# Layer 0's context attention and its FFN in one phase of a two-layer decoder kernel

## The chip, the cores and the metric

The kernel runs on one core of a Trainium2 chip. The metric is the device time of one execution in microseconds (us). The engines are named as the profile names them: PE (TensorE matmul), PEld (TensorE weight load), DVE (VectorE), ACT (ScalarE), POOL (GpSimd), SP (SyncE, which here only issues DMAs; its queue is SPq).

## The reference, cut to what matters

A decoder of two layers over 8 batches of 512 tokens of width 256, all float32. Each sublayer is followed by a residual add and a layer norm. The change touches two sublayers of layer 0: attention over a context of 64 keys per batch, and an FFN whose two butterfly transforms the kernel folds into its two weight matrices beforehand.

```python
# x: (8, 512, 256)   ctx: (8, 64, 256)
x = layernorm(x + L0_attn(x))                      # self attention, 16 heads of 16

def L0_xattn(q, k, v, mask):                       # q = x, k = v = ctx, 16 heads of 16
    sim = einsum('bhqd,bhkd->bhqk', q, k) / sqrt(16)
    sim = sim + (-1e9) * (1 - mask)
    out = einsum('bhqk,bhkd->bhqd', softmax(sim), v)
    return out                                     # heads side by side, no projection
x = layernorm(x + L0_xattn(x, ctx, ctx, mask))

def L0_ffn(x):
    h = x @ W_exp + b_exp                          # 256 -> 1024
    h = gelu(butterfly(h, up_weights) + up_bias)
    h = butterfly(h, down_weights)
    return h @ W_con + b_con + down_bias           # 1024 -> 256
x = layernorm(x + L0_ffn(x))
# layer 1: causal self attention (16 heads of 64), attention over tokens and context,
# and a mixture of 8 experts (2 per token) that scatters tokens into rows by expert
```

## The kernel before

The kernel is one program traced in Python. Instructions of one engine run in their order in that engine's queue. That order is set when the program is built: a planner walks the traced instructions, those traced earlier having priority, and gives an engine the next one that its own estimate of times calls ready, so an instruction can stand ahead of work that was traced before it. At run time nothing is reordered, and an engine whose next instruction isn't ready waits.

Activations stay in SBUF as `xs[b]`, one tile of 128 x (4 x 256) per batch, and each sublayer overwrites it. Tiles come from pools. A *phase* is a pool that is opened for one stage; where its tiles lie over tiles of an earlier phase, each waits for the tiles that it lies over (`reuse_waits="tile"`). The pool `routing` (variable `keep`) is an ordinary one and is opened after layer 0's FFN; it holds the small tables of the expert routing and the zero tile from which the expert rows in DRAM (`rows_in`, 64 DMAs from SP, line 781) are cleared. PSUM, from this point on, is split into three kinds of tiles with two buffers each: `s` (two banks; scores, hidden units, Q/K), `t` (one bank; transposes) and `o` (one bank; products).

`_pipeline(units, stages, later)` runs a list of units through stages, one step apart: in step n stage k works on unit n - k. After the stages of each step it runs one piece of the list `later`.

**Context attention** (phase `l0_context`, lines 637 to 724). A unit is a block of 128 queries of a batch, so there are 32 units, and four stages:

- `l0x_pre`, once per batch: x transposed to `xT` (8 transposes on PE, copied out by DVE and ACT); `bd`, the keys spread block-diagonally so that 8 heads are one matmul (2 POOL multiplies, line 643); the mask by DMA (`mi`, line 650) turned into a bias; `v2`, the values of head pairs with zeros between them (a POOL memset, line 654, and two DMAs, line 656). `bd` uses the tag `att` of the pool `work`, which the self attention ahead of it and other stages use too.
- `l0x_scores`: two matmuls of 512 columns (line 666, each recorded as two) into an `s` tile; then on DVE scale and bias (675), row maxima (683), subtraction (684); Exp on ACT (685); sums on DVE (686).
- `l0x_transposes`: 8 transposes of the probabilities (696), copied out half by DVE (94) and half by ACT (96).
- `l0x_values`: 8 narrow matmuls with `v2` (705, 16 records); reciprocal, scaling (711) on DVE, residual on POOL (717); after a batch's last unit the norm (199 to 209), which writes `xs[b]`.

**FFN** (phase `l0_ffn`, lines 727 to 763). First the down weights are transposed (`wdn`, line 761). Then a pipeline over the 8 batches with two stages. `ffn_up` transposes `xs[b]`, makes 8 blocks of 128 hidden units in four `s` tiles (line 738, 32 records per batch), and applies Gelu on ACT (747) into `g`, a tile of 16 KB per partition with two buffers. `ffn_down` multiplies by `wdn` (`project_and_norm`, line 225, 64 records per batch) into `o` tiles, adds x plus the bias row (232), and norms.

Layer 1's self attention (`l1_self`, lines 783 to 912) follows. It is a pipeline over 256 units (batch, head pair, query block) in which Q, K and V of the next head pair are made while the present one is worked on. The rotary turn of Q and K ends with four accumulating DMAs from POOL per head pair (`qk<-turned`, line 810), for which that pair's first scores (855) wait.

The DMAs of layer 1's attention weights (lines 625 to 634) are traced just before the context attention.

Of the kernel before, what the change touches and what calls it, by code (L numbers as in the profile page):

```python
# [11 lines left out]
F32 = mybir.dt.float32  # L12
I32 = mybir.dt.int32
AF = mybir.ActivationFunctionType
ALU = mybir.AluOpType
# [3 lines left out]
P = 128  # L19
S = 512  # L20
D = 256
S2 = 64
NT = S // P
KC = D // P
# [3 lines left out]
BLK = 256  # L28


def _pipeline(units, stages, later=None):


    units = list(units)
    for step in range(len(units) + len(stages) - 1):
        for k, stage in enumerate(stages):
            if 0 <= step - k < len(units):
                stage(*units[step - k])
        if later:
            later.pop(0)()  # L40
    while later:
        later.pop(0)()

# [2 lines left out]
def decoder_kernel(ctx: ExitStack, tc: tile.TileContext, a: dict, out: bass.AP):  # L46
    nc = tc.nc
    NB = a["x"].shape[0]
# [23 lines left out]
    def phase(name):  # L72

        return tc.tile_pool(name=name, bufs=2, side="right", reuse_waits="tile")
# [10 lines left out]
    def o_tile(name):  # L85
        return pp["o"].tile([P, 512], F32, tag="o", name=name)
# [35 lines left out]
    def rows(w):  # L122

        return w.rearrange("(c p) n -> p c n", p=P)
# [62 lines left out]
    def x_transposed(b):  # L187
        xT = work.tile([P, KC, S], F32, tag="xT", name="xT")
        transposed(xT, xs[b])
        return xT  # L190

    def normed(dst, r, on_act=False):

        st = work.tile([P, NT, 6], F32, tag="st", name="st")
        mv = work.tile([P, NT, 2], F32, tag="mv", name="mv")
        ve = work.tile([P, NT], F32, tag="ve", name="ve")
        rs = work.tile([P, NT], F32, tag="rs", name="rs")
        for i in range(NT):
            dve.bn_stats(st[:, i, :], r[:, i, :])  # L199
            dve.bn_aggr(mv[:, i, :], st[:, i, :])  # L200
        dve.tensor_scalar(ve, mv[:, :, 1], LN_EPS, None, ALU.add)
        pool.tensor_tensor(rs, ve, mhalf, ALU.pow)
        if on_act:
            dve.scalar_tensor_tensor(ve, mv[:, :, 0], -1.0, rs, ALU.mult, ALU.mult)
        for i in range(NT):
            if on_act:
                act.activation(dst[:, i, :], r[:, i, :], AF.Identity, bias=ve[:, i : i + 1], scale=rs[:, i : i + 1])
                continue
            dve.tensor_scalar(
                dst[:, i, :], r[:, i, :], mv[:, i, 0:1], rs[:, i : i + 1], ALU.subtract, ALU.mult  # L210
            )

    def r_tile():
        return work.tile([P, NT, D], F32, tag="r", name="r", bufs=1)

    def project_and_norm(b, lhs, w, n, plus, later=None):

        r = r_tile()

        def piece(i2):  # L220
            o = o_tile("o_out").rearrange("p (i n) -> p i n", i=2)
            for j in range(2):
                i = 2 * i2 + j
                for c in range(n):
                    pe.matmul(  # L225
                        o[:, j, :],
                        lhsT=lhs[:, c, i * P : (i + 1) * P],
                        rhs=w[:, c, :],
                        start=(c == 0),
                        stop=(c == n - 1),  # L230
                    )
            dve.tensor_tensor(r[:, 2 * i2 : 2 * i2 + 2, :], o, plus[:, 2 * i2 : 2 * i2 + 2, :], ALU.add)
            if i2 == NT // 2 - 1:
                normed(xs[b], r)

        for i2 in range(NT // 2):
            if later is None:
                piece(i2)
            else:
                later.append(partial(piece, i2))  # L240
# [101 lines left out]
    live = {}  # L342
# [191 lines left out]
    with tc.tile_pool(name="bfly", bufs=1, side="right") as bfly, phase("l0_self") as ph, psum("a", 3, 1, 1):  # L534
# [25 lines left out]
        later = []  # L560
# [60 lines left out]
    cs = tabs[:, 0:1024].rearrange("p (t n) -> p t n", t=2)  # L621
    causal = tabs[:, 1024:1536]


    sp.dma_start(out=wqT, in_=rows(a["at_wqT"]))
    sp.dma_start(out=wkdT, in_=rows(a["at_wkdT"]))
    sp.dma_start(out=wkuT, in_=a["at_wkuT"])
    sp.dma_start(out=wvuT, in_=a["at_wvuT"])

    sp.dma_start(out=cs[:, 0, :], in_=a["rope"][0])  # L630
    for h in range(0, P, 32):
        sp.dma_start(out=cs[h : h + 32, 1, :], in_=a["rope"][1][h ^ 32 : (h ^ 32) + 32, :])
    sp.dma_start(out=causal, in_=a["causal"])
    sp.dma_start(out=woT1, in_=rows(a["at_woT"]))

    def l0x_pre(b, i):
        if i:
            return
        xT = x_transposed(b)

        bd = work.tile([P, KC, 8, S2], F32, tag="att", name="bd")
        for c in range(KC):
            pool.tensor_tensor(
                bd[:, c],
                ctxT[:, c, b * S2 : (b + 1) * S2].unsqueeze(1).to_broadcast([P, 8, S2]),
                hmask.unsqueeze(2).to_broadcast([P, 8, S2]),
                ALU.mult,
            )
        mi = ph.tile([P, NT, S2], I32, tag="mi", name="mi")
        sp.dma_start(out=mi, in_=a["mask"][b].rearrange("(i p) k -> p i k", p=P))  # L650
        bias = ph.tile([P, NT, S2], F32, tag="bias", name="bias")
        dve.tensor_scalar(bias, mi, 1.0, 1.0e9, ALU.subtract, ALU.mult)
        v2 = ph.tile([P, 8, 32], F32, tag="v2", name="v2")
        pool.memset(v2, 0.0)
        for j in range(2):
            sp.dma_start(
                out=v2[64 * j : 64 * (j + 1), :, 16 * j : 16 * (j + 1)],
                in_=a["ctx"][b * S2 : (b + 1) * S2, :].rearrange("k (h two n) -> k h two n", two=2, n=16)[:, :, j, :],
            )
        live["xT", b], live["bd", b], live["bias", b], live["v2", b] = xT, bd, bias, v2  # L660

    def l0x_scores(b, i):
        xT, bd, bias = live["xT", b], live["bd", b], live["bias", b]
# [35 lines left out]

    def l0x_values(b, i):  # L700
        pt, sums = live.pop(("pt", b, i))
        v2 = live["v2", b]
        o = o_tile("o_xpv")
        for h in range(8):
            pe.matmul(o[:, h * 32 : (h + 1) * 32], lhsT=pt[:, h, :], rhs=v2[:, h, :], start=True, stop=True)
        rsum = col("rsum16", 16)
        dve.reciprocal(rsum, sums)
        if i == 0:
            live["r", b] = r_tile()
        r = live["r", b]  # L710
        dve.tensor_tensor(
            r[:, i, :].rearrange("p (h n) -> p h n", h=16),
            o[:, 0:D].rearrange("p (h n) -> p h n", h=16),
            rsum.unsqueeze(2).to_broadcast([P, 16, 16]),
            ALU.mult,
        )
        pool.tensor_tensor(r[:, i, :], r[:, i, :], xs[b][:, i, :], ALU.add)
        if i == NT - 1:
            normed(xs[b], r)

    with phase("l0_context") as ph:
        _pipeline(
            [(b, i) for b in range(NB) for i in range(NT)], [l0x_pre, l0x_scores, l0x_transposes, l0x_values]
        )


    def big_tile(name, bufs=1):
        return ph.tile([P, 8, S], F32, tag="big", name=name, bufs=bufs)

    def ffn_up(b):  # L730
        xT = x_transposed(b)
        g = big_tile("g", 2)
        for f2 in range(4):
            s = s_tile("s_h")
            for j in range(2):
                f = 2 * f2 + j
                for c in range(KC):
                    pe.matmul(
                        s[:, j, :],
                        lhsT=wup[:, c, f * P : (f + 1) * P],  # L740
                        rhs=xT[:, c, :],
                        start=(c == 0),
                        stop=(c == KC - 1),
                    )
            for j in range(2):
                f = 2 * f2 + j
                act.activation(g[:, f, :], s[:, j, :], AF.Gelu, bias=upb[:, f : f + 1])
        xb = work.tile([P, NT, D], F32, tag="att", name="xb")
        pool.tensor_tensor(xb, xs[b], dnb.unsqueeze(1).to_broadcast([P, NT, D]), ALU.add)
        live["g", b] = g, xb  # L750

    def ffn_down(b):
        g, xb = live.pop(("g", b))
        project_and_norm(b, g, wdn, 8, xb)

    with phase("l0_ffn") as ph:
        wdn = ph.tile([P, 8, D], F32, tag="wdn", name="wdn", bufs=1)
        for f in range(0, 8, 2):
            t = t_tile("tW")
            for j in range(4):  # L760
                pe.transpose(t[:, j, :], wdnT[:, j % 2, (f + j // 2) * P : (f + j // 2 + 1) * P], ident)
            evac(wdn[:, f : f + 2, :].rearrange("p f n -> p (f n)"), t.rearrange("p j n -> p (j n)"))
        _pipeline([(b,) for b in range(NB)], [ffn_up, ffn_down])

# [75 lines left out]
            dve.tensor_scalar(p[:, j, 0:n], p[:, j, 0:n], rsum[:, j : j + 1], None, ALU.mult)  # L842

    put_off = []

    def nothing(*_):
        pass

    def l1_scores(b, c, i):
        q, k, _ = live["qkv", b, c]  # L850
# [545 lines left out]
```

## Time and profile before

| what | value |
|---|---|
| time, median of 3 runs | 4053.77 us (4045.73 to 4060.90) |
| profiled execution | 4058.26 us, its span 4056.5 us |
| PE busy over the span | 3799.6 us (94%) |
| DVE / ACT / POOL busy | 2195.0 / 1418.2 / 1098.8 us |
| mean granted TensorE clock | 0.947 |
| context attention, 912 to 1146 us of the span | PE busy 203.54, DVE busy 217.56 of 234 us, clock 0.75 |
| FFN, 1158 to 1384 us | PE busy 225.96, DVE busy 44.44 of 226 us, clock 1.00 |
| loads of an activation table on ACT | 4 in the whole span, 1283 ns each |

A busy PE is not PE at full speed: the table gives the clock that was granted beside it. The profile names a group by source line, engine, operation and tiles; a line can be that of a helper (184 transposes, 94 and 96 copies out of PSUM, 199 to 209 the norm). [...]

### The profile page before, as it was taken

The numbers are of one execution on the slowest core, as the hardware profiler recorded it, in microseconds if no ns is written. First come the engines' busy times: TensorE is split into PE (matmuls) and PEld (weight loads), VectorE is DVE, ScalarE is ACT, GpSimd is POOL, SyncE is SP. The second block draws the span as 40 slices with busy tenths as digits, with TensorE's granted clock in tenths as the row PEclk, the third lists the DMA queues.
The fourth block names the chain that finished last, engine by engine and source line by source line (L and its number), as shares of the span: only waits on it lengthen the run. The fifth ranks groups of instructions, "written<-read, shape, count | busy, mean of one in ns | idle before, by whom it ended". The sixth has DMA issues, their size and how long they took to land. (4 is left out here: it accounts for less than half of the span.)

```text
span 4056.5 us, 58011 instructions
## 1 busy us (share of the span) xinstructions
PE 3799.6 (94%) x22164; PEld 2393.7 (59%) x22164; DVE 2195.0 (54%) x6177; ACT 1418.2 (35%) x2980; POOL 1098.8 (27%) x974
## 2 busy tenths in 40 slices
PE   8999999998999999999999999999999995999995
PEld 3333333346656655666566665666666664888884
DVE  5666656558942377777777765555555553000002
ACT  2443343442221254444544433333333331222222
POOL 4767566652211122211211110110101101122222
PEclk8999899997789999999999999999999997999997
DMA  3000011119500122222322220000000001766664
GB/s 120 25 22 22 22 32 32 32 52 236 124 6 1 32 37 32 32 32 32 40 35 32 32 32 1 17 13 10 12 17 17 17 11 40 243 183 182 182 183 107
DMA packets 173432, 236.12 MB, mean 58 GB/s; under 512 B 26554, under 2 KB 138618, under 8 KB 173155
## 3 DMA queue, kind: packets, MB, share of 16 engines
q1 hardware_dynamic: 146562, 179.93, 14.6%
q0 software_dynamic: 26592, 52.49, 9.0%
q8 instruction: 175, 2.87, 0.3%
q14 instruction: 103, 0.84, 0.1%
HBM read 136.78 MB, written 62.03 MB: 49 GB/s over the span
## 5 line engine op out<-in xcount | busy, mean ns | idle before, releaser
L417 DVE CUSTOM_DVE_ANT_0 scored<-s_sc,decay 128x512 f32<-128x512 f32 x512 | 323.4, 687 | 293.4 <-PE s_sc L412 291.9
L470 ACT ACTIVATE pt<-s_st 128x1024 f32<-128x1024 f32 x256 | 261.4, 1024 | 373.0 <-PE o_pv L481 224.9
L810 POOL DMA_DIRECT2D qk<-turned x256 | 202.6, 1207 | 627.0 <-issue 273.0
L96 ACT COPY pt<-tP 128x128 f32<-128x128 f32 (+2 forms) x480 | 224.3, 467 | 384.2 <-PE tP L279 299.2
L279 PE MATMUL tP<-ident,p 128*128 128x128 f32 x2304 | 355.5, 287 | 2.3 <-DVE pt L94 0.8
L279 PEld LDWEIGHTS tP<-ident,p 128*128 128x128 f32 x2304 | 250.6, 143 | 145.8 <-issue 74.0
L269 ACT ACTIVATE p<-p,nm 128x128 f32<-128x128 f32 (+3 forms) x512 | 283.0, 555 | 145.4 <-DVE nm L267 145.4
L983 ACT ACTIVATE p<-s_sc,nm 128x576 f32<-128x576 f32 x256 | 189.6, 743 | 348.9 <-DVE nm L982 348.9
L1287 DVE TENSOR_SCALAR y<-o_y,share 128x256 f32<-128x256 f32 x78 | 34.2, 479 | 491.8 <-PE o_y L1265 491.8
L842 DVE TENSOR_SCALAR p<-p,rsum 128x576 f32<-128x576 f32 (+4 forms) x768 | 295.4, 428 | 6.1
L1249 PE MATMUL s_h<-xnT,we 128*128 128x256 f32 x1248 | 284.7, 381 | 2.8 <-DMA we<-in_mo_w 2.8
L412 PE MATMUL s_sc<-k,q 32*128 32x512 f32 x1024 | 267.5, 703 | 16.4 <-ACT k L398 14.0
L94 DVE COPY pt<-tP 128x128 f32<-128x128 f32 (+2 forms) x480 | 259.1, 540 | 42.5 <-PE tP L279 28.6
L257 DVE CUSTOM_DVE_ANT_0 p<-s_sc,tabs 128x128 f32<-128x128 f32 (+3 forms) x512 | 234.9, 484 | 84.9 <-PE s_sc L855 84.9
L855 PE MATMUL s_sc<-qk 64*128 64x128 f32 (+3 forms) x1024 | 265.8, 486 | 12.3 <-DVE turned L807 8.2
L1265 PE MATMUL o_y<-we,h 128*128 128x256 f32 x1248 | 275.6, 379 | 0.0
L1265 PEld LDWEIGHTS o_y<-we,h 128*128 128x128 f32 x1248 | 237.1, 190 | 32.2
L1249 PEld LDWEIGHTS s_h<-xnT,we 128*128 128x128 f32 x1248 | 232.6, 191 | 32.2 <-DMA we<-in_mo_w 3.2
L982 DVE TENSOR_REDUCE nm<-s_sc 128x1 f32<-128x576 f32 x256 | 183.6, 749 | 119.1 <-PE s_sc L981 119.1
L1288 POOL DMA_INDIRECT total<-y,to x78 | 121.2, 1554 | 458.5 <-DVE y L1287 295.1
L891 PE MATMUL o_pv<-pt,vc 128*64 128x128 f32 x2560 | 221.8, 284 | 0.0
L1007 PE MATMUL o_pv<-pt,vc 128*64 128x128 f32 x2048 | 197.7, 287 | 0.0
(248 smaller groups left out, 6476.1 us busy)
## 6 DMA issues: line engine op xcount, KB each, us to landing
we<-in_mo_w SPq DMA_DIRECT2D x78, 1024.0 KB, 5.7
rows_in<-zero SPq DMA_DIRECT2D x64, 530.0 KB, 11.2
qk<-turned POOLq DMA_DIRECT2D x256, 128.0 KB, 4.4
xr<-rows_in SPq DMA_DIRECT2D x39, 265.0 KB, 6.2
coef<-in_ff_upw SPq DMA_DIRECT2D x40, 256.0 KB, 3.2
coef<-in_ff_dnw SPq DMA_DIRECT2D x40, 256.0 KB, 3.1
x<-in_x SPq DMA_DIRECT2D x8, 512.0 KB, 9.4
total<-x SPq DMA_DIRECT2D x8, 512.0 KB, 2.9
```

What stands on the lines that cost most here:

```text
L94: dve.tensor_copy(dst, src)
L96: act.copy(dst, src)
L257: dve.tensor_tensor_reduce(out=p[:, j, 0:n], in0=s[:, j, 0:n], in1=m, scale=1.0, scalar=-3.0e38, op0=op, op1=reduced, accum_out=mx[:, j : ...
L269: act.activation(p[:, j, 0:n], p[:, j, 0:n], AF.Exp, bias=nm[:, j : j + 1], scale=scale, accum_out=sums[:, at + j : at + j + 1],)
L279: pe.transpose(t[:, k, :], p[:, j, k * P : (k + 1) * P], ident)
L412: pe.matmul(s[:, j, :], lhsT=q[h : h + 32, i * P : (i + 1) * P], rhs=k[h : h + 32, :], start=True, stop=True)
L417: dve.tensor_tensor_reduce(out=scored[:, h, :], in0=s[:, j, :], in1=decay[:, i, :], scale=1.0, scalar=-3.0e38, op0=ALU.mult, op1=ALU.max, ...
L470: act.activation(pt, s, AF.Exp, scale=1.0 / 16.0)
L842: dve.tensor_scalar(p[:, j, 0:n], p[:, j, 0:n], rsum[:, j : j + 1], None, ALU.mult)
L855: pe.matmul(s[:, j, 0:n], lhsT=q[h : h + 64, i * P : (i + 1) * P], rhs=k[h : h + 64, 0:n], start=True, stop=True)
L1249: pe.matmul(s[:, j, :], lhsT=w1[:, c, f * P : (f + 1) * P], rhs=xnT[:, c, :], start=(c == 0), stop=(c == KC - 1),)
L1265: pe.matmul(o[:, i, :], lhsT=h[:, f, i * P : (i + 1) * P], rhs=w2[:, f, :], start=(f == 0), stop=(f == 7),)
```

## The change

The two phases become one, `l0_context_ffn`. Its tiles are opened together:

- `v2` is one tile for all 8 batches (8 KB per partition), cleared once and filled by 16 DMAs ahead of the pipeline; `l0x_pre` no longer makes it.
- The FFN of a batch is cut into 7 pieces: `start` (transpose of x), four `up` (one `s` tile and its two Gelus each) and two `down` (one `o` tile each, the second with the norm). When a batch's context attention has been normed, `l0x_values` appends them, with one empty piece ahead (two for the first batch), to the list `behind`.
- `_pipeline` takes two pieces of that list after the stages of each step. A batch has 4 steps and 8 pieces. So the FFN of batch b is traced among the attention steps of the batches after it, and the last one after all attention.
- `g` becomes 6 buffers of 4 KB instead of two of 16 KB; the attention's result tile gets its own buffer (`rx`), and `bd` its own tag, in the phase.
- `wdn` is transposed at the head of the phase, and layer 1's weight DMAs are traced after `v2`'s.

By the shapes of its tiles the new phase takes 77,824 bytes per partition (`v2` 8192, `wdn` 8192, `bd` 8192, `mi` and `bias` 2048 each, `p` 12288, `pt` 8192, `rx` 4096, `g` 24576); the phase `l0_self` and the pool `bfly` ahead of it, in whose bytes it lies, take 76,800 together.

```diff
-def _pipeline(units, stages, later=None):
+def _pipeline(units, stages, later=None, pieces=1):
...
-        if later:
-            later.pop(0)()
+        for _ in range(pieces):
+            if later:
+                later.pop(0)()
     while later:
         later.pop(0)()
...
-    sp.dma_start(out=wqT, in_=rows(a["at_wqT"]))
...
+    def weights_of_layer_1():
+        sp.dma_start(out=wqT, in_=rows(a["at_wqT"]))
...
     def l0x_pre(b, i):
...
-        bd = work.tile([P, KC, 8, S2], F32, tag="att", name="bd")
+        bd = ph.tile([P, KC, 8, S2], F32, tag="bd", name="bd")
...
-        v2 = ph.tile([P, 8, 32], F32, tag="v2", name="v2")
-        pool.memset(v2, 0.0)
-        for j in range(2):
-            sp.dma_start(out=v2[64 * j : 64 * (j + 1), :, 16 * j : 16 * (j + 1)], ...
...
     def l0x_values(b, i):
...
-            pe.matmul(o[:, h * 32 : (h + 1) * 32], lhsT=pt[:, h, :], rhs=v2[:, h, :], start=True, stop=True)
+            pe.matmul(o[:, h * 32 : (h + 1) * 32], lhsT=pt[:, h, :], rhs=v2[:, b, h, :], start=True, stop=True)
...
-            live["r", b] = r_tile()
+            live["r", b] = ph.tile([P, NT, D], F32, tag="rx", name="rx", bufs=1)
...
         if i == NT - 1:
             normed(xs[b], r)
+            behind.extend(([nothing] if b == 0 else []) + [nothing] + ffn(b))
+
+    behind = []
...
-    def ffn_up(b):
-        xT = x_transposed(b)
-        g = big_tile("g", 2)
-        for f2 in range(4):
+    def ffn(b):
+        def start():
+            live["xT", b] = x_transposed(b)
+
+        def up(f2):
+            xT = live["xT", b]
             s = s_tile("s_h")
...
+            g = ph.tile([P, 2, S], F32, tag="g", name="g", bufs=6)
             for j in range(2):
                 f = 2 * f2 + j
-                act.activation(g[:, f, :], s[:, j, :], AF.Gelu, bias=upb[:, f : f + 1])
...
+                act.activation(g[:, j, :], s[:, j, :], AF.Gelu, bias=upb[:, f : f + 1])
+            live["g", b, f2] = g
+
+        def down(i2):
+            if i2 == 0:
+                xb = work.tile([P, NT, D], F32, tag="att", name="xb")
+                pool.tensor_tensor(xb, xs[b], dnb.unsqueeze(1).to_broadcast([P, NT, D]), ALU.add)
+                live["down", b] = xb, r_tile()
...
+                for f in range(8):
+                    pe.matmul(o[:, j, :], lhsT=live["g", b, f // 2][:, f % 2, i * P : (i + 1) * P], rhs=wdn[:, f, :], ...
+            dve.tensor_tensor(r[:, 2 * i2 : 2 * i2 + 2, :], o, xb[:, 2 * i2 : 2 * i2 + 2, :], ALU.add)
+            if i2 == NT // 2 - 1:
+                normed(xs[b], r)
+
+        return [start] + [partial(up, f2) for f2 in range(4)] + [partial(down, i2) for i2 in range(2)]
+
+    with phase("l0_context_ffn") as ph:
+        v2 = ph.tile([P, NB, 8, 32], F32, tag="v2", name="v2", bufs=1)
+        pool.memset(v2, 0.0)
+        for b in range(NB):
+            for j in range(2):
+                sp.dma_start(out=v2[64 * j : 64 * (j + 1), b, :, 16 * j : 16 * (j + 1)], ...
+        weights_of_layer_1()
         wdn = ph.tile([P, 8, D], F32, tag="wdn", name="wdn", bufs=1)
...
-        _pipeline([(b,) for b in range(NB)], [ffn_up, ffn_down])
+        _pipeline(
+            [(b, i) for b in range(NB) for i in range(NT)],
+            [l0x_pre, l0x_scores, l0x_transposes, l0x_values],
+            behind,
+            pieces=2,
+        )
```

More of the change, by code (lines that the diff above doesn't have):

```diff
@@ L622, in decoder_kernel, with nothing @@
     causal = tabs[:, 1024:1536]
-    sp.dma_start(out=wqT, in_=rows(a["at_wqT"]))
[L626 to L634, printed above, removed]
+    def weights_of_layer_1():
+        sp.dma_start(out=wqT, in_=rows(a["at_wqT"]))
+        sp.dma_start(out=wkdT, in_=rows(a["at_wkdT"]))
+        sp.dma_start(out=wkuT, in_=a["at_wkuT"])
+        sp.dma_start(out=wvuT, in_=a["at_wvuT"])
+        sp.dma_start(out=cs[:, 0, :], in_=a["rope"][0])
+        for h in range(0, P, 32):
+            sp.dma_start(out=cs[h : h + 32, 1, :], in_=a["rope"][1][h ^ 32 : (h ^ 32) + 32, :])
+        sp.dma_start(out=causal, in_=a["causal"])
+        sp.dma_start(out=woT1, in_=rows(a["at_woT"]))
+    def nothing(*_):
+        pass
     def l0x_pre(b, i):
@@ L652, in l0x_pre @@
         dve.tensor_scalar(bias, mi, 1.0, 1.0e9, ALU.subtract, ALU.mult)
-        v2 = ph.tile([P, 8, 32], F32, tag="v2", name="v2")
-        pool.memset(v2, 0.0)
-        for j in range(2):
[L656 to L660, printed above, removed]
+        live["xT", b], live["bd", b], live["bias", b] = xT, bd, bias
     def l0x_scores(b, i):
@@ L701, in l0x_values @@
         pt, sums = live.pop(("pt", b, i))
-        v2 = live["v2", b]
         o = o_tile("o_xpv")
         for h in range(8):
-            pe.matmul(o[:, h * 32 : (h + 1) * 32], lhsT=pt[:, h, :], rhs=v2[:, h, :], start=True, stop=True)
+            pe.matmul(o[:, h * 32 : (h + 1) * 32], lhsT=pt[:, h, :], rhs=v2[:, b, h, :], start=True, stop=True)
         rsum = col("rsum16", 16)
@@ L719, in l0x_values @@
             normed(xs[b], r)
[L721 to L724, printed above, removed]
+            behind.extend(([nothing] if b == 0 else []) + [nothing] + ffn(b))
+    behind = []
     def big_tile(name, bufs=1):
         return ph.tile([P, 8, S], F32, tag="big", name=name, bufs=bufs)
-    def ffn_up(b):
-        xT = x_transposed(b)
-        g = big_tile("g", 2)
-        for f2 in range(4):
+    def ffn(b):
[3 more added lines that the diff above has]
+            xT = live["xT", b]
             s = s_tile("s_h")
@@ L744, in ffn_up @@
                     )
+            g = ph.tile([P, 2, S], F32, tag="g", name="g", bufs=6)
             for j in range(2):
                 f = 2 * f2 + j
-                act.activation(g[:, f, :], s[:, j, :], AF.Gelu, bias=upb[:, f : f + 1])
[L748 to L756, printed above, removed]
+                act.activation(g[:, j, :], s[:, j, :], AF.Gelu, bias=upb[:, f : f + 1])
[5 more added lines that the diff above has]
+                live["down", b] = xb, r_tile()
+            xb, r = live["down", b]
+            o = o_tile("o_out").rearrange("p (i n) -> p i n", i=2)
+            for j in range(2):
+                i = 2 * i2 + j
+                for f in range(8):
+                    pe.matmul(
+                        o[:, j, :],
+                        lhsT=live["g", b, f // 2][:, f % 2, i * P : (i + 1) * P],
+                        rhs=wdn[:, f, :],
+                        start=(f == 0),
+                        stop=(f == 7),
+                    )
[7 more added lines that the diff above has]
+        for b in range(NB):
+            for j in range(2):
+                sp.dma_start(
+                    out=v2[64 * j : 64 * (j + 1), b, :, 16 * j : 16 * (j + 1)],
+                    in_=a["ctx"][b * S2 : (b + 1) * S2, :].rearrange("k (h two n) -> k h two n", two=2, n=16)[:, :, j, :],
+                )
+        weights_of_layer_1()
         wdn = ph.tile([P, 8, D], F32, tag="wdn", name="wdn", bufs=1)
@@ L762, in decoder_kernel, with big_tile @@
             evac(wdn[:, f : f + 2, :].rearrange("p f n -> p (f n)"), t.rearrange("p j n -> p (j n)"))
-        _pipeline([(b,) for b in range(NB)], [ffn_up, ffn_down])
+        _pipeline(
[3 more added lines that the diff above has]
+            pieces=2,
+        )
+    def big_tile(name, bufs=1):
+        return ph.tile([P, 8, S], F32, tag="big", name=name, bufs=bufs)
     dram = ctx.enter_context(tc.tile_pool(name="dram", bufs=1, space=bass.MemoryType.DRAM))
@@ L844, in decoder_kernel @@
     put_off = []
-    def nothing(*_):
-        pass
     def l1_scores(b, c, i):
```

## The prediction

> **What bounds the kernel now.** I read the 40 slices first, to find the stages; then the busy times by stretch; then groups and the order of time inside each stage; last the waits of POOL and SP. By stretch (busy us and instructions of PE, PEld, DVE, ACT, POOL, then the granted clock):
>
> ```profile
> 912.00:1146.00 234.00, 203.54 (x957) 153.23 (x956) 217.56 (x346) 59.27 (x76) 57.99 (x69) 0.75 0.66 156
> 1158.00:1384.00 226.00, 225.96 (x819) 150.86 (x820) 44.44 (x117) 45.77 (x72) 21.23 (x13) 1.00 0.02 8
> 1547.00:2400.00 853.00, 844.08 (x5328) 507.76 (x5325) 626.42 (x2190) 390.68 (x1177) 176.10 (x219) 1.00 0.27 35
> ```
>
> The reader is to see two neighbours with opposite bounds. The context attention (first line) is DVE's: once it runs, DVE is busy 165.71 of the 167 us from 969 to 1136. PE's 203.54 busy us are inflated, at a clock of 0.75. The FFN (second line) is PE's alone at clock 1.00, with DVE idle four fifths of the time. The third line is layer 1's self attention, where pieces of different work are already mixed on PE: 99% busy, clock 1.00.
>
> DVE's work per attention unit, from the groups between 910 and 1146 us (busy us, mean ns):
>
> ```profile
> L684 DVE TENSOR_TENSOR p<-p,mx 128x1024 f32<-128x1024 f32 x32 | 46.3, 1449 | 0.0
> L686 DVE TENSOR_REDUCE sums<-p 128x16 f32<-128x1024 f32 x32 | 38.7, 1212 | 1.9 <-ACT p L685 1.4
> L683 DVE TENSOR_REDUCE mx<-p 128x16 f32<-128x1024 f32 x32 | 38.6, 1209 | 0.0
> L675 DVE SCALAR_TENSOR_TENSOR p<-s_xs,bias 128x1024 f32<-128x1024 f32 x32 | 38.2, 1197 | 0.0
> ```
>
> Four passes take 161.8 us; with copies, scaling and norms DVE needs 217.56/32 = 6.8 us per unit.
>
> PE's real price is read where it runs undisturbed, in the order of time (start, length of the stretch, count at the end):
>
> ```profile
> 940.50 3.46 PE L705 MATMUL o_xpv<-v,pt 128*128 128x32 f32 x16
> 976.74 1.87 PE L705 MATMUL o_xpv<-v,pt 128*128 128x32 f32 x16
> 979.39 1.04 PE L696 MATMUL tP<-ident,p 128*128 128x128 f32 x8
> 1173.61 13.04 PE L738 MATMUL s_h<-xT,wup 128*128 128x512 f32 x30
> 1186.49 13.54 PE L225 MATMUL o_out<-wdn,g 128*128 128x256 f32 x62
> ```
>
> The first two lines are the same 16 matmuls at half and at full clock.
>
> [...] 3.46 against 1.87 us above, mean clock 0.75 in the stage with PE gaps, 1.00 in those without. [...] line 684 takes 1.22 us, but 1.87 and 3.13 us beside POOL's `bd` and `xb`; these stay. [...]
>
> **The change, part by part.**
>
> *PE, the sum.* At full clock a unit costs 4 score records at 13.04/30 = 0.435, so 1.74, plus 1.04 and 1.87: 4.65 us. 32 units are 149, and 8 transposes of x at 1.04 are 8: 157 us where 234 are spent now. The FFN is 226, `wdn` 2. Together 385 us for the 472 from 912 to 1384. DVE has 217.56 + about 55 = 273 us of work, ACT 110: so in one phase PE bounds, at 46 us per batch (4 units, one x, 28.3 of FFN) against 34 of DVE. This is the gain: DVE's attention hides behind FFN matmuls.
>
> *The head is not overlapped.* FFN 0 needs `xs[0]`, which was normed at 969; until then only DVE-bound attention exists. DVE's first softmax pass came at 923.7 because of waits of POOL and SP:
>
> ```profile
> SPq L650 <- PE o_out L525: 25.1, 1, 25.1
> POOL bd L643 <- PE tT L517: 22.9, 1, 22.9
> POOL inumbers L774 <- PE o_out L525: 3.0, 1, 3.0
> ```
>
> The mask DMA waited 25.1 us for the self attention's last product, and a `bd` 22.9 us for the buffer `att`, with the `v2` memset queued behind it on POOL. `bd` now has its own tag and `mi` other bytes. I don't know over which tiles these lie: bounds 0 to 12 us earlier (self attention's own matmuls run until 907); I take 9, so FFN 0 begins at 960. By then PE has done 7 units, two transposed x and `wdn`: 37 us. Left: 348.
>
> *PE's efficiency in the mix.* Bounds: 100% (FFN now) and 80%, if tile turnover costs each step 3 us. The nearest row is layer 1's 99% busy by records, which flatters. I take 95%: 366 us. A tail of 4 us follows (the last norm before FFN 7, mostly covered by FFN 6's last piece). End 960 + 366 + 4 = 1330 instead of 1384: 54 us less.
>
> *`v2`.* Eight memsets of 0.31 become one of about 2.5 us on POOL, ahead of nothing due there; 16 DMAs at 0.62 us are 10 us of SP in one piece. The memset must wait for old tiles, at the latest those read until 907. The first values came at 935, so some 15 us are spare; if `mi` of batch 0 fell behind these DMAs, the 9 us above would go. POOL's later waits for `o_xpv` (35.0 us for 6 memsets) vanish but delayed nobody on the path.
>
> *Layer 1's weight DMAs* move behind `v2`'s on SP. They are first read at 1385; 400 us of cover, cost nothing.
>
> *`wdn`.* 16 transposes and 4 copies move into the head, where PE has gaps: about 1.4 us of DVE.
>
> *Table loads.* Gelus come in about three bursts per batch, each between Exps: 6 loads x 8 = 48 (32 to 64), times 1.283 = 62 us on ACT. ACT rises to some 172 of 418 us. What waits: an Exp, then PE's transposes; FFN matmuls stand between. [...] so I put it at 0, within the 95%.
>
> *Two `s` and two `o` buffers* now serve both works. A step's order on PE is scores (1.74), transposes (1.04), values (1.87), two pieces (3.5 each); a score tile must be read by line 675 within 6.4 us, a hidden tile by two Gelus (1.27, with a load 2.55) within 3.5. It fits on average, not in every order: part of the 5%.
>
> *The clearing of `rows_in`.* `inumbers` and the zero tile waited for line 525, the last reader of the phase `l0_self`: the pool `routing` lies in its bytes. The new phase reaches 1 KB lower still, so `routing` must wait for its end, about 1330. Then 64 DMAs, which filled the engines from 925 to about 1070, run beside layer 1's self attention:
>
> ```profile
> rows_in<-zero SPq DMA_DIRECT2D x64, 530.0 KB, 11.2
> qk<-turned POOLq DMA_DIRECT2D x256, 128.0 KB, 4.4
> ```
>
> Behind `qk<-turned` stand PE's scores of that head pair, and all behind them on PE. A pair takes 13.5 us; in the order of time (1560 to 1580) its last DMA issues at 1571.7 and scores come at 1579.1: 7.4 us, of which 4.4 are used. Upper bound: it lands like the clearing itself, 11.2, so (11.2 - 7.4) x 145/13.5 = 41 us. Lower: the accumulating POOL DMAs of the experts land in 4.7 (at most 7.7) beside weights at 183 GB/s, so 0. I take 8.
>
> **Sum.** -54 + 8 = -46 us, on the profiled execution's 4058.3 (span 4056.5 and 1.8 around it): 4012. The median of the runs is 4.5 us lower, so 4008.
>
> **The rivals.** About 0.5% (20 us) is what a measurement here can tell from no change.
>
> *Little is gained: turnover.* PE's queue holds a fixed order, planned on estimates. If it stands wrongly, PE waits for line 675, which queues on DVE behind sums that wait for an Exp and its table load. For: `s_xs` once waited 4.8 us for 675. Against: layer 1 mixes the same three kinds of PSUM tiles, two buffers each, and PE idles 1% there. At 85%: 409, end 1373, -11 + 8: about 4050.
>
> *Slower: the clearing starves the turn.* One mechanism, place and price as above. With the gain of 54 it decides from 54/10.7 = 5 us of stall per pair, a landing of 12.4 us; with a landing of 16 the stalls are 92 us and the result +38: 4092. For: clearing DMAs landed in up to 12.6 us with several outstanding. [...]
>
> *It doesn't do what it says*: the planner keeps FFN pieces behind all attention. Then only the head's 9 us and the clearing remain: 4053. Against: PE idles beside DVE-bound units, and pieces have priority over later steps.
>
> **How the numbers follow.** Forecast (PE-bound, 90 to 100%) 0.66; turnover 0.17; starved 0.11; not interleaved 0.06. Best: no loss, no clearing cost, head 12: -79, so 3975. The range's upper end takes in the little-gain cases and some starving: 4065. Faster by over 0.5% (below 4033): 0.66 plus 0.02 of turnover = 0.68. Within: 0.19. Slower (above 4074): 0.13, which adds 0.02 of turnover worse than 80%.
>
> **What would show it.** Right: from about 965 to 1330 PE is near full at clock above 0.95, DVE near 75%; about 48 table loads; the first line 675 near 914; the clearing after 1320; layer 1 starts near 1330. Wrong: clock near 0.75 in the merged stretch, PE waiting for 675 or Gelu; or, with the phase short as said, scores of line 855 waiting for `qk<-turned` for tens of us.

## The result and the profile after

| | before | after |
|---|---|---|
| time, median of 16 runs each | 4054.44 us (4045.73 to 4063.41) | 4022.09 us (4012.00 to 4040.06) |
| profiled execution, its span | 4058.26, 4056.5 us | 4032.56, 4030.8 us |
| mean granted TensorE clock | 0.947 | 0.956 |
| activation table loads on ACT in layer 0's context attention and FFN | 1 | 39 |

The ratio of the runs is 0.9921, with a 95% interval of 0.9908 to 0.9935: 32 us or 0.8% faster. The forecast was 4008 us, with a range of 3975 to 4065.

Line numbers of the kernel after: score matmuls 664; scale and bias 673, maxima 681, subtraction 682, Exp 683, sums 684; transposes 694; values 702; FFN up 736, Gelu 746, FFN down 759; `wdn`'s transposes 786; `bd` 648; clear of `v2` 774; clearing of `rows_in` 814; layer 1's scores 885.

The busy times by stretch of after (length, then busy us and instructions of PE, PEld, DVE, ACT, POOL; then the granted clock, DMA share, GB/s). The first stretch has only the first batch's attention, the second both works mixed, the third the last batch's FFN:

```profile
929.00:976.00 47.00, 40.69 (x184) 31.66 (x182) 41.10 (x58) 11.09 (x16) 9.24 (x8) 0.73 0.00 1
977.00:1309.00 332.00, 320.55 (x1447) 219.75 (x1446) 206.47 (x373) 133.17 (x158) 55.45 (x55) 0.97 0.01 2
1309.00:1347.00 38.00, 37.49 (x155) 27.02 (x155) 9.45 (x30) 5.64 (x9) 5.38 (x6) 1.00 0.00 1
```

The pair of opposite stages of before (DVE 217.56 of 234 us at clock 0.75; PE 225.96 of 226 at 1.00) has become one stretch with PE busy 320.55 of 332 us at clock 0.97 and DVE at 206.47 of 332, 62%. Only the first batch's 47 us still look like the old attention stage: clock 0.73, DVE 41.10 of 47.

DVE's groups between 929 and 1347 us of after (busy us, mean ns, idle before them and its releaser):

```profile
L682 DVE TENSOR_TENSOR p<-p,mx 128x1024 f32<-128x1024 f32 x32 | 39.0, 1219 | 0.5
L684 DVE TENSOR_REDUCE sums<-p 128x16 f32<-128x1024 f32 x32 | 38.8, 1212 | 34.6 <-ACT p L683 34.6
L673 DVE SCALAR_TENSOR_TENSOR p<-s_xs,bias 128x1024 f32<-128x1024 f32 x32 | 38.4, 1200 | 10.3 <-PE s_xs L664 10.3
```

The same 32 passes at the same price, but now DVE waits: 34.6 us for the Exp, 10.3 us for scores. It is no longer the one that sets the pace. ACT's groups in the same window show the price that the mixing pays:

```profile
L683 ACT ACTIVATE p<-p 128x1024 f32<-128x1024 f32 x32 | 33.8, 1057 | 25.8 <-DVE p L682 25.6
L746 ACT ACT_TABLE_LOAD x20 | 25.7, 1283 | 0.3
L683 ACT ACT_TABLE_LOAD x19 | 24.4, 1283 | 22.6 <-DVE p L682 22.3
```

**Where the time went**, from the order of time of both profiled executions. The last transpose of the self attention (`tO`) starts at 907.56 us before and 909.61 after; all that follows is measured from there.

| stretch | before | after | difference |
|---|---|---|---|
| start to the last `tO` | 907.56 | 909.61 | +2.1 |
| last `tO` to DVE's first softmax pass | 16.1 | 19.4 | +3.3 |
| first softmax pass to the FFN's last matmul | 460.7 | 417.5 | -43.2 |
| FFN's last matmul to layer 1's first scores | 14.5 | 19.0 | +4.5 |
| layer 1's first to last scores | 996.5 | 1003.8 | +7.3 |
| rest of the span | 1661.1 | 1661.6 | +0.5 |

The sum is -25.5 us on two single executions; the medians differ by 32.4. Single executions of these two kernels scatter over 18 and 28 us, so single stretches are compared below and not whole spans.

The last two pluses are the clearing of `rows_in`. The issues of after (KB each, median us to landing), then the waits of POOL for the end of the phase and of layer 1's scores for the turned keys (us in total, times, longest; the last line is of before):

```profile
rows_in<-zero SPq DMA_DIRECT2D x64, 530.0 KB, 11.7
qk<-turned POOLq DMA_DIRECT2D x256, 128.0 KB, 4.5
```

```profile
POOL inumbers L807 <- PE o_out L759: 25.9, 1, 25.9
PE s_sc L885 <- DMA qk<-turned: 12.6, 7, 7.8
PE s_sc L855 <- DMA qk<-turned: 3.9, 2, 3.4
```

The zero tile's pool now waits for the FFN's last product, and the 64 DMAs start at 1348.7 us, into layer 1's self attention, where they stood at 925 before. The waits for turned keys grow from 3.9 us (2 times) to 12.6 (7 times). The median of 4.5 us says little about the clearing's effect: it is taken over all 256 transfers, and only 40 of them were issued beside the clearing. Taken apart (issued from 1348 to 1490 us, then from 1490 to 2400) they read:

```profile
qk<-turned POOLq DMA_DIRECT2D x40, 128.0 KB, 9.2
qk<-turned POOLq DMA_DIRECT2D x216, 128.0 KB, 4.4
```

Beside the clearing the median landing doubles, from 4.4 to 9.2 us, and the longest goes from 6.5 to 14.0.

### The profile page after: what moved, and what is told of

The parts are those of the page before. It is cut to its first block, busy times and chain, and to the rows that moved or that the text cites. A ratio compares the mean times of both kernels' runs of the same rounds, so it can differ in the third digit from the quotient of the medians.

```text
span 4030.8 us, 57975 instructions
## 1 busy us (share of the span) xinstructions
PE 3774.7 (94%) x22164; PEld 2369.8 (59%) x22164; DVE 2187.6 (54%) x6177; ACT 1464.5 (36%) x3018; POOL 1093.6 (27%) x967
## 5 line engine op out<-in xcount | busy, mean ns | idle before, releaser
L885 PE MATMUL s_sc<-qk 64*128 64x128 f32 (+3 forms) x1024 | 268.5, 486 | 20.9 <-DMA qk<-turned 12.6
L413 PE MATMUL s_sc<-k,q 32*128 32x512 f32 x1024 | 266.6, 699 | 16.3 <-ACT k L399 14.0
## 6 DMA issues: line engine op xcount, KB each, us to landing
rows_in<-zero SPq DMA_DIRECT2D x64, 530.0 KB, 11.7
```

Source lines behind the costliest of these rows:

```text
L413: pe.matmul(s[:, j, :], lhsT=q[h : h + 32, i * P : (i + 1) * P], rhs=k[h : h + 32, :], start=True, stop=True)
L885: pe.matmul(s[:, j, 0:n], lhsT=q[h : h + 64, i * P : (i + 1) * P], rhs=k[h : h + 64, 0:n], start=True, stop=True)
```

## The experiments

The times are medians, and the ratios compare with runs of the kernel before in the same session. One table holds the stretches that the verdicts rest on; "end" is the FFN's last matmul, "scores" those of layer 1.

| kernel | `tO` to first pass | first pass to first FFN matmul | from there to end | end to first scores | first to last scores |
|---|---|---|---|---|---|
| after | 19.4 | 48.0 | 369.6 | 19.0 | 1003.8 |
| e1_wdn_later | 21.0 | 44.4 | 368.2 | 18.1 | 1000.0 |
| e9_v2_after_bd | 19.4 | 48.0 | 369.6 | 18.7 | 1001.6 |
| e2_clear_early | 21.4 | 43.8 | 368.5 | 14.5 | 997.1 |
| e10_all_three | 17.1 | 46.1 | 369.9 | 14.6 | 996.0 |
| e4_not_mixed | 19.4 | 223.6 | 232.2 | 18.4 | 1001.8 |
| e5_no_gelu_table | 19.4 | 48.0 | 383.0 | 18.4 | 1004.9 |
| before | 16.1 | 234.4 | 226.3 | 14.5 | 996.5 |
| e6_no_shift_before | 16.1 | 202.2 | 226.3 | 14.4 | 997.2 |
| e7_no_shift_after | 19.4 | 31.7 | 350.1 | 19.0 | 1003.2 |
| e13_no_shift_clear_early | 19.4 | 31.7 | 353.6 | 14.5 | 996.6 |

**Is it the mixing?** The same phase, but no piece of the FFN is taken between attention steps:

```diff
-            pieces=2,
+            pieces=0,
```

> The changed kernel with pieces=0: all tiles and the head as in the change, but every FFN piece is traced after all attention. Theory A (the whole gain is DVE's attention hidden behind FFN matmuls): the stage is as long as before plus the longer head and the clearing in layer 1, so slower than before by 5 to 25 us (ratio 1.001 to 1.006), attention stretch with clock near 0.75, FFN stretch with 1.00. Rival B (part of the gain is values laid out once, bd out of att, or shorter waits of POOL): faster than before by 10 us or more. Rival C (the planner mixes by itself, since DVE-bound attention leaves PE idle): clock above 0.9 in the attention stretch and a time near the changed kernel's.

Measured: 4068.29 us, ratio 1.0034 [1.0019, 1.0050]. The two stages are apart again (columns as above):

```profile
931.00:1154.00 223.00, 190.96 (x957) 143.82 (x957) 211.19 (x336) 57.64 (x74) 51.51 (x53) 0.79 0.01 3
1154.00:1387.00 233.00, 229.95 (x827) 152.71 (x827) 46.65 (x124) 45.63 (x72) 22.27 (x15) 0.99 0.00 1
```

DVE is busy 211.19 of 223 us at clock 0.79, then PE 229.95 of 233 at 0.99. So everything else in the change costs 14 us (0.34%), and taking the pieces between the steps is worth 46 us: 4068 to 4022. In the traces 38.2 of the 46 us lie between the first pass and the FFN's end (223.6 + 232.2 against 48.0 + 369.6); where the rest lies they don't show. The 14 us are themselves a sum. The head, the FFN and the clearing cost more than in before, but the stretch up to the first FFN matmul is 10.8 us shorter (223.6 against 234.4). Of that, 6.4 lie in the attention itself, from the first pass to the end of its last value matmul (221.1 against 227.5 us), as much as DVE's 32 subtractions took less (39.9 against 46.3); the rest lies between the two stages, where before transposes `wdn`.

**What bounded the old attention stage, and what bounds the mix?** Two kernels leave out the softmax's shift in layer 0's context attention, two of DVE's four passes; one starts from before, one from after. The edit is the same:

```diff
-        dve.tensor_reduce(mx, p, AX.X, ALU.max)
-        dve.tensor_tensor(p, p, mx.unsqueeze(2).to_broadcast([P, 16, S2]), ALU.subtract)
```

> Leaves out the shift of layer 0's context softmax (the max reduce and the subtract of its maximum) in the kernel BEFORE; Exp is taken of the unshifted scores. Two of VectorE's four passes of a 6.8 us attention unit go, 32 units in all. Theory A (VectorE bounds the old attention phase, VectorE and TensorE hand over at a low clock): the phase falls from about 218 us to TensorE's own 157 us at full clock or a little above, so the kernel gains 45 to 60 us (ratio about 0.986 to 0.989), about as much as the mixing brought. Theory B (the old phase was bound by TensorE at its lower clock, VectorE only looked busy): gain under 10 us.

Measured: 4030.36 us, ratio 0.9945 [0.9925, 0.9965], 21 us gained. Neither theory's number. The attention stage of that kernel:

```profile
929.00:1128.00 199.00, 179.69 (x962) 137.82 (x963) 139.10 (x276) 57.53 (x76) 48.95 (x60) 0.82 0.66 182
```

DVE is down to 139.10 of 199 us and no longer the bound, and the stage shrinks by 32 us (234.4 to 202.2), 11 more than the medians of the runs, a difference that the traces don't explain. But PE doesn't come to its own rate: it is busy 90% of the time by records, at a clock of 0.82. 179.69 us at 0.82 is 147 us of work at full clock, so 52 of the 199 us are gaps and the low clock. Relieving the busiest engine gave less than half of the way from 234 to the 157 us of PE's work at full clock.

> The same two VectorE passes left out in the kernel AFTER (unshifted Exp). Theory A (in the mixed stretch TensorE is the bound, at 96% busy, and VectorE is under it): only the first batch's 8 units, which run before any FFN piece, get shorter, by some 1 to 2 us each: 8 to 16 us gained on the kernel after, 4 us more at most from VectorE's waits in the mixed stretch. Theory B (VectorE still sets the pace of the mixed stretch and TensorE is only stretched by it): 40 us or more gained. So the same edit is worth about 50 us before the change and about 12 after it under A, and about the same in both under B.

Measured: 3987.23 us, ratio 0.9845 [0.9820, 0.9870], about 31 us less than after by the two ratios. In the trace the phase is 35.7 us shorter: 16.3 before the first FFN matmul, as theory A said, and 19.5 in the mixed part, where it had said 4 at most. After's mixed part was therefore not as close to PE's rate as 97% busy by records suggests. The traces divide the 19.5 us: PE was idle for 12.0 us of the mixed part in after and for 2.9 here, and the clock took 10.6 and 1.6 us, if each stretch of the clock's record is counted with its length times (1 - granted clock). In after the largest of PE's waits, in total, was that of the hidden matmuls for DVE's copy of the transposed x; here it is nearly gone (after, then e7):

```profile
PE s_h L736 <- DVE xT L95: 8.6, 6, 1.6
PE s_h L734 <- DVE xT L95: 0.5, 1, 0.5
```

The edit is worth 32 us in the phase before and 36 after, so what the change gives and what the edit gives add up. But in both kernels without the shift the traces show PE, DVE and ACT running their instructions in another order than in the kernel that they start from. No run parts what the lighter DVE gave from what the planner's new order gave. Without the shift the change saves (202.2 + 226.3) - (31.7 + 350.1) = 46.7 us, with it 43.2. The stretch by stretch view of the mixed part without the shift:

```profile
966.00:1290.00 324.00, 321.06 (x1502) 225.37 (x1502) 157.17 (x337) 132.26 (x159) 60.53 (x59) 1.00 0.01 2
```

PE is busy 321.06 of 324 us at clock 1.00. This is what PE as the bound looks like.

**Who holds the head?** In after, x of the first batch is transposed at 925.5 us where before had it at 906.8. In the order of time (start, us; in brackets idle before and its releaser), three things stand ahead of the first softmax pass of after:

```profile
909.00 1.81 POOL L774 MEMSET v<- 128x2048 f32 x1 [15.04 <-PE o_pv L482]
910.76 4.04 POOL L648 TENSOR_TENSOR bd<-ctxT,small 128x512 f32<-128x512 f32 x4
...
924.14 0.66 PE L786 MATMUL tW<-ident,wdnT 128*128 128x128 f32 x4 [0.94 <-DVE wdn L95]
...
925.47 1.09 PE L185 MATMUL tT<-ident,x 128*128 128x128 f32 x8 [0.68 <-ACT wdn L97]
925.82 1.02 POOL L203 TENSOR_TENSOR rs<-ve,mhalf 128x4 f32<-128x4 f32 x1 [11.02 <-DVE ve L202]
```

The clear of `v2` waits 15.04 us for the self attention's last product, with `bd` behind it on POOL; `wdn`'s transposes stand ahead of x's on PE and wait for copies out of PSUM; and the self attention's last norm (`rs`) comes just as late. Three kernels undo the first two, singly and then together. First the transposes, as the first piece behind the second batch's attention:

```diff
-        for f in range(0, 8, 2):
-            t = t_tile("tW")
...
+        def lay_wdn():
+            for f in range(0, 8, 2):
+                t = t_tile("tW")
...
-            behind.extend(([nothing] if b == 0 else []) + [nothing] + ffn(b))
+            behind.extend(([live["lay_wdn"]] if b == 0 else []) + [nothing] + ffn(b))
```

> The changed kernel with one edit: wdn's 16 transposes and 4 copies are no longer traced at the head of the phase but as the first piece behind the attention, in the place of an empty one. Theory A (the head went wrong because wdn's transposes take the t tiles and DVE/ACT ahead of x's first transposes, so the first scores came at 927 instead of 910 and the first softmax pass at 929 instead of 924): first pass of line 673 between 919 and 923, xs[0] normed 7 to 10 us earlier, the end of the FFN and the whole 7 to 10 us earlier (ratio to before about 0.990). Rival B (the head waits for the self attention's last product and norm on DVE, whatever stands on PE): first pass within 2 us of 929, no change of the time. Rival C (the head gets shorter, but wdn then delays FFN 0 by as much): first pass earlier, end of the FFN the same.

Measured: 4021.9 us, ratio 0.9922 [0.9901, 0.9944], no change against after's 0.9921. x is transposed at 910.42 as hoped, yet the first pass comes later (21.0 us after `tO`), since the planner now puts most of `bd` behind the norm on POOL, and PE waits for that:

```profile
928.29 1.02 POOL L203 TENSOR_TENSOR rs<-ve,mhalf 128x4 f32<-128x4 f32 x1 [14.93 <-DVE ve L202]
929.28 3.21 POOL L648 TENSOR_TENSOR bd<-ctxT,small 128x512 f32<-128x512 f32 x3
...
930.38 4.11 PE L664 MATMUL s_xs<-bd,xT 128*128 128x512 f32 x5 [2.67 <-POOL bd L648]
```

That is a part of it only. The clock was at half speed here from 913.6 to 927.3 us (in after from 912.7 to 919.6), so that the second half of the self attention's last product took 3.78 us instead of 1.99, and the norm behind it ended later too.

Then the clear of `v2` and its DMAs, traced behind the first batch's `bd` instead of ahead of the pipeline:

```diff
-        pool.memset(v2, 0.0)
-        for b in range(NB):
...
+        if b == 0:
+            live["lay_v2"]()
```

> The value layout's clear and its DMAs are put behind the laying out of batch 0's keys on GpSimd, nothing else. The keys' layout no longer stands behind the clear that waits 15 us for the self attention, so it is done near 900 us instead of 915. Theory A (the keys' layout alone holds the first scores): first scores at about 912 us instead of 927, first softmax pass at about 922, kernel 5 to 8 us faster than after. Theory B (the transposes of the FFN's down weights, ahead of x's on TensorE, hold the first scores as well): scores stay at 926 to 927 us, kernel within 3 us of after.

Measured: 4028.17 us, ratio 0.9940 [0.9920, 0.9961], no gain; theory B. Half of `bd` is ready at 894 us, where after has its first instruction of it at 910.76, behind the clear, but the first pass stays 19.4 us after `tO`, because x's transposes are still behind `wdn`'s and the last norm is as late as in after: DVE waits only 1.75 us for the scores once the norm is done. Then both, with the early clearing of the next experiment:

> Three edits on the kernel after: the value layout's clear behind batch 0's key layout, the down weights' transposes as the first piece behind the second batch's attention, and the zero tile in a dead weight's place so that the clearing of the buffer rows runs at 930 to 1050 us. Theory A (in the head three things stood one behind the other, keys' layout, weight transposes, last norm of the self attention on VectorE until about 923 us): first softmax pass at about 923 us instead of 929, FFN's end about 5 us earlier, and the early clearing gives its 12 us beside it: 15 to 20 us faster than after, about 4004 us. Theory B (the norm before it or another wait keeps the head as it is): 12 us faster than after, like the early clearing alone, about 4010 us.

Measured: 4017.48 us, ratio 0.9904 [0.9882, 0.9927]. The first pass comes 17.1 us after `tO`, 2.3 us sooner than in after, and the first FFN matmul at 63.2 instead of 67.4: 4 us. About half of these are not owed to the two edits of the head, since e2_clear_early below, which has neither, has 65.2; and the time is no better than that kernel's 4010.34. Theory A's 6 us for the pass and 15 to 20 us for the time didn't come; on theory B's 12 the runs don't decide. What is left in the head is the norm. DVE's queue in **before** already shows it, in the stretch where the prediction read a wait for the mask:

```profile
912.43 1.87 PE L666 MATMUL s_xs<-bd,xT 128*128 128x512 f32 x2
...
917.44 0.69 DVE L528 TENSOR_TENSOR r<-o_out,x 128x512 f32<-128x512 f32 x1 [6.82 <-PE o_out L525]
...
920.22 0.69 DVE L528 TENSOR_TENSOR r<-o_out,x 128x512 f32<-128x512 f32 x1 [1.08 <-PE o_out L525]
...
923.26 0.16 DVE L204 SCALAR_TENSOR_TENSOR ve<-mv,rs 128x4 f32<-128x4 f32 x1 [0.98 <-POOL rs L202]
923.34 0.28 DVE L652 TENSOR_SCALAR bias<-mi 128x256 f32<-128x256 int32 x1
923.66 2.36 DVE L675 SCALAR_TENSOR_TENSOR p<-s_xs,bias 128x1024 f32<-128x1024 f32 x2
```

The first pass (675) starts right behind the self attention's last norm (528 to 204) on the same queue. The mask's bias (652) takes 0.28 us in between; in this order of the queue the pass could not have started 1 us sooner, had the mask been there at 900. Another order might have let it: the first score tile was made by 914.3 (the second pair of its matmuls is the first line), and DVE stood idle for 6.82 us until 917.44. A queue with the pass ahead of the norm was not tried; with the mask early, the planner didn't write one in any of the kernels here.

**The clearing.** The zero tile takes the place of a dead weight of the self attention instead of lying in the pool that waits for the phase, and its last column is made by an iota that needs no table of the pool:

```diff
-    zero = keep.tile([P, ROW], F32, name="zero")
+    zero = wo0.rearrange("p c n -> p (c n)")[:, 0:ROW]
...
-    dve.tensor_copy(zero[:, D + NE : D + NE + 1], tokens_at[:, NB * NT : NB * NT + 1])
+    dve.tensor_copy(zero[:, D + NE : D + NE + 1], past_all)
```

> The changed kernel with one edit: the zero tile that clears rows_in is made in the weight tile wo0, which is dead after layer 0's self attention, instead of in the pool routing, so that the 64 clearing DMAs can start at about 922 as in the kernel before. Theory A (the clearing beside layer 1's self attention costs 12 us there: 5 in its first turn, 7 in the first ten head pairs): from the last FFN product to the last scores of line 885 (23 + 1001 us in the changed kernel) becomes 17 + 995, and the whole is 12 us shorter, unless masks late behind the clearing on SP take it back. Rival B: the 12 us are the order of instructions or chance, not the clearing; layer 1 stays at 1001. Rival C (masks): masks of batches 2 to 4 land 10 to 20 us late behind 24 to 28 clearing DMAs in one piece, line 657 waits, and the merged stretch gets 5 to 20 us longer.

Measured: 4010.34 us, ratio 0.9896 [0.9874, 0.9918]: 12 us less than after by the medians, 10 by the ratios (whose intervals overlap a little). The trace decides. The clearing's DMAs are issued from 932.3 to 1047.8, the mixed part isn't longer for it (368.5 us), and both stretches of layer 1 are back where before had them: 14.5 and 997.1 us against 19.0 and 1003.8. The waits of layer 1's scores:

```profile
PE s_sc L887 <- DMA qk<-turned: 4.7, 2, 3.3
```

So the clearing costs 4.5 + 6.7 = 11 us in after. Every kernel of the table with the late clearing shows 18.1 to 19.0 in the column before last, every one with the early clearing 14.4 to 14.6.

**The price of the table loads.** Identity in Gelu's place (the nonlinearity is left out); the expectation reckons with the loads alone:

```diff
-                act.activation(g[:, j, :], s[:, j, :], AF.Gelu, bias=upb[:, f : f + 1])
+                act.activation(g[:, j, :], s[:, j, :], AF.Identity, bias=upb[:, f : f + 1])
```

> The changed kernel with Identity in the place of Gelu (it leaves out the FFN's nonlinearity; Identity takes the same time per instruction and needs no table of its own), so that the 39 table loads between Exp and Gelu go. Theory A (the loads are hidden behind PE in the mixed stretch): time within 5 us of the changed kernel's, stretch from the first hidden matmul to the last down product 369 us as there, give or take 4. Rival B (each load delays an Exp or frees an s tile late, and PE waits): 39 x 1.28 = 50 us of ACT, of which at least a third, 15 us or more, comes off the stretch.

Measured: 4040.46 us, ratio 0.9972 [0.9959, 0.9986], slower than after by 18 us with all 39 loads gone. The planner knows the loads and wrote a different order for PE, DVE and ACT, and with it the mixed part takes 383.0 us instead of 369.6, at clock 0.93. PE's idle time there is nearly that of after (13.2 and 12.0 us); what grew is the time that the clock took (27.6 and 10.6 us, counted as above). The experiment doesn't price the loads. Since Identity takes as long as Gelu (684 and 685 ns) and nothing else was edited, the order is the likely cause of the 13 us, but it was not varied by itself. For the loads the trace of after shows the direct waits: in the mixed part PE waited for ACT's Exp or Gelu 3.3 us in all (2.2 and 1.1), and its weight loads 8.1 (5.6 and 2.5). What reached PE by way of DVE, which itself waited 34.6 us for the Exp, is not in them; all of PE's idle time there is 12.0 us. The loads themselves took 1283 ns each: 33 of the 39 start 17 to 19 ns after the instruction before them, and behind 31 the next one starts 11 or 12 ns later.

**The best version.** e2_clear_early beats both kernels and leaves nothing out. With the shift left out as well:

> The kernel after with two edits together: layer 0's context softmax without its shift (max reduce and subtract left out) and the zero tile in a dead weight's place, so that the buffer rows are cleared at 930 to 1050 us. Theory A (the two costs lie in different stretches and add): 12 us on top of what leaving out the shift gave (3987 us), so about 3975 us, a ratio of 0.981 to the kernel before; layer 1's first scores wait 3.3 us for their turned keys instead of 7.9. Theory B (the transfers of the clearing, which now run under a faster first batch and its mask, slow that stretch): 3980 to 3990 us, with the first FFN matmul later than 32 us after the first softmax pass.

Measured: 3986.20 us, ratio 0.9832 [0.9805, 0.9859], not to be told from e7_no_shift_after's 0.9845. In the trace the clearing's part is there: 4.5 and 6.6 us less in the two stretches of layer 1, as in e2, against 3.5 us more in the mixed part. There the clock of this execution has one more stretch at half speed, 6.8 us from 1012.2, which is worth 3.4. The stage after layer 1's self attention, where PE's order is the same in both, took 10 us less in the profiled execution of e7 than in those of e13 and after. Most of that is the clock too: it took 83 us there in e7, 93 in e13 and 91 in after, counted as above.

## Why the prediction was right, and where it was not

- **The gain, its mechanism and its size in the mixed part: right.** It said that DVE's attention hides behind FFN matmuls, with 366 us for the mix at 95% and a tail of 4, 370 in all from batch 0's norm to the end. It took 374.0 (972.5 to 1346.5), and 369.6 from the first FFN matmul. e4_not_mixed shows that it is the mixing, and the rival "not interleaved" falls with it; "turnover", at 409 us for the mix, falls with the 369.6. The 5% allowed for order was needed: PE was idle for 12.0 us of the mix, most of it for DVE's copies of x, and the clock took 10.6. e7 got 18 of these back, by a lighter DVE or by its other order. DVE was busy for 62% of the mix, where 75 was said. One sum is off without harm: by its own figures a batch costs PE 48 us (4 x 4.65 + 1.04 + 28.3) and not 46, while the total of 385 is right.
- **The head: the step that failed.** It said that the first pass "came at 923.7 because of waits of POOL and SP" and took 9 us for their going. The mask wait did go (its DMA issued at 897.2 instead of 920.25), but the pass came 3.3 us later after `tO`, not 9 earlier. Two errors. The wait named was hidden beside the last norm, which ended with it and stands ahead of the pass on DVE. And the things that the change put into the head were priced by their duration, not by what queues behind them: the clear of `v2` was said to be "ahead of nothing due" on POOL, while `bd` stood behind it; `wdn` was said to move "where PE has gaps" at 1.4 us of DVE, while its copies out of PSUM held the tiles that x's transposes needed. Undoing both (e10) gives 2.3 of the 3.3 us back, so the larger part of the miss, some 10 us, is the forecast gain. It wasn't to be had in the orders that the planner wrote; whether another order has it stays open.
- **The clearing: mechanism right, size 8 for 11 us.** It did move behind the phase's end (POOL's wait of 25.9 us) and beside layer 1, as said. The 8 were picked between bounds of 0 and 41, so that they came near is partly luck. The term was sized by landings over 7.4 us in a steady pipeline. Beside the clearing the median landing was 9.2, which by the prediction's formula, (9.2 - 7.4) x 145/13.5, makes 19 us; the scores lost 7.3. Another 4.5 came at a place that the term left out, layer 1's very first scores, which have nothing before them to hide a late landing. The rival in which the clearing starves the turn (landings of 16, 92 us; its weight of 0.11 was the author's estimate) is out: the longest landing was 14.0.
- **Table loads: 48 said, 39 found, one at each of the 39 changes between Exp and Gelu in the trace of after; the cost, by the author's estimate 0 within the 95%, stays unmeasured.** The direct waits were 3.3 us on PE and 8.1 on its weight loads.
- **"These stay": not so.** The slow subtractions beside POOL (up to 3.31 us in before) are gone: the longest of 32 takes 1226 ns in after. 46.3 became 39.0 us, a small gain on DVE that the sum left out. In before eight of the 32 ran beside POOL's `bd` or `xb`, the seven slow ones among them: five took 1.87 to 2.00 us beside `bd`, two 3.13 and 3.31 beside `xb`, all others 1.18 to 1.22. In after one ran beside `xb`, for 1.05 us, and took 1.22.
- **`v2`'s waits, layer 1's weight DMAs: costless, as said.** POOL's 35.0 us of waiting for `o_xpv` are gone. e4_not_mixed, which has lost them too, is no faster as a whole; its attention is 6.4 us shorter, but the subtractions account for these. With the clearing out of the way layer 1's first scores come 14.5 us after the FFN, as before, so its weights are there in time.
- **The clock: as read from before.** The argument counted PE's work in the mix at full clock, since the stage with gaps on PE had 0.75 and those without 1.00. The runs show the same pairing: 0.73 with the first batch's attention alone (PE busy 40.69 of 47 us), 0.97 in the mix (320.55 of 332), 0.82 in e6 with a relieved DVE (179.69 of 199). What sets the clock they don't show. A less busy DVE alone did not close PE's gaps in e6; a second work in PE's queue did in the mix.

Counted from the last `tO`, the phase's end came 39.9 us earlier (+3.3 and -43.2) and not 54, and the clearing cost 11 and not 8. With these the sum is -29 us, beside a difference of 32 between the medians.

## What to carry to other kernels

Fill the gaps of a stage that is paced by one engine with another stage's matmuls rather than only relieve that engine: here leaving out two of DVE's four softmax passes saved 32 us of the phase, the change 43, and both together 79 (460.7 to 381.8). Before a wait is counted as a gain, look at what else ends at that moment in the queue of the engine that waits; and before an instruction is put "where there is room", look at who stands behind it on its own queue. When a phase's bytes grow, follow which later pool lies in them and what that pool starts: here a zero tile sent 34 MB of DMAs into another stage for 11 us, and a dead weight's place took it back.

## What the runs showed of the hardware that I had not expected

- Beside the clearing on SP's queue (64 transfers of 530 KB, landing in 11.7 us), 40 small transfers from POOL's queue (128 KB) landed in 9.2 us in the median (6.6 to 14.0), against 4.4 for the 216 behind it. The median over all 256, 4.5, hides that.
- A stage with PE busy 90% by records still ran at a granted clock of 0.82 (e6), one busy 97% at 0.97, one busy 99% at 1.00. The busy share by records hides what the clock takes: at 0.82 the 90% are 74% of PE at full speed.
- Nearly the same idle time of PE stood beside very different amounts of clock: 13.2 us idle in the mix of e5 went with 27.6 us taken by the clock, 12.0 in that of after with 10.6.
